# Softmax sums of an attention kernel on column quarters of the array: one reciprocal of 256 columns and eight products of 32 rows

## The chip, the cores and the metric

The kernel runs on one core of a Trainium2 chip. The metric is device time in microseconds (us) for one execution; the median of 3 runs of the kernel before is 2319.12 us (2315.53 to 2322.49).

## The reference

One transformer layer on x of 16 sequences x 512 tokens x 256 features, all in float32. First causal attention with 16 heads of 64 features, with the scores clamped by a tanh, and then a mixture of 8 experts (the best 2 of each token) beside one shared expert. Cut to what matters here:

```python
x = x + attn(layernorm(x));  x = x + ffn(layernorm(x))

def attn(x):                                  # per sequence: 512 tokens, 16 heads of 64
    q, k, v = (heads(x @ W.T) for W in (Wq, Wk, Wv))
    sim = 50 * tanh(q @ k.T / 8 / 50)
    attn = softmax(where(causal, sim, min))   # exp, divided by its sum over the keys
    return (attn @ v) @ Wo.T

def ffn(t):
    shared = gelu(t @ sw1 + sb1) @ sw2 + sb2
    p, i = top_k(softmax(t @ gate_w + gate_b), 2)
    routed = sum over the two of p * (gelu(t @ w1[i] + b1[i]) @ w2[i] + b2[i])
    return routed + shared
```

## The kernel before

**Attention.** Sequences (b, 0 to 15) and within each the eight pairs of heads (p, 0 to 7) are one stream of 128 steps. A pair's two heads (i = 0, 1) occupy partitions 0 to 63 and 64 to 127 wherever features lie on partitions. Scores are kept transposed: keys on partitions, queries along the free dimension, so the softmax sum over keys is a sum over partitions, which a product with a matrix of ones gives.

For each pair there are these parts. `project_qk` (L244) makes q and k with eight full-array matmul instructions of 512 columns (`pq`, L249; each float32 product is two instructions in the trace), copied to SBUF by ScalarE (L256). `score_matmuls` (L264) makes the scores in three units of key blocks, `s` at L272, with 64 rows of the array for either head. `exponentials` (L283) runs tanh and exp on ScalarE (L287, L288), masks the diagonal blocks on GpSimd (L291) and adds the key blocks of a pair on GpSimd (`added`, L303 to L310) for queries 128 to 511; for queries 0 to 127 only key block 0 counts. `attend` (L314) multiplies by the values into the PSUM tile `av` (L323; 64 columns of the array for either head), and then makes the sums, repeated over a head's 64 partitions, in the PSUM tile `sums` of 128 x 512 (L332). VectorE takes two reciprocals of 256 columns from `sums` into `oT` (L342) and multiplies `oT` by `av` over 512 columns (L343). `av` and `sums` have one buffer each, so the next pair's `av` matmuls can't begin before L343 has read this pair's.

**Order.** TensorE's order is written out by hand (L826 to L839): at step s come the score units 0 and 1 of the pair s + 1, then `attend` of the pair s, score unit 2 of s + 1, `early`, `project_qk` of s + 2, and `around`. The other engines' orders are made by a scheduler when the program is built; each engine works its own queue in order.

What stands between the attention steps depends on p. At p = 0 and 1 comes the output projection of the sequence before (`po`, L353), then at p = 1 its second layernorm. At p = 2 come the first layernorm of the next sequence (L186: statistics on VectorE, the power on GpSimd at L196, four normalising instructions on VectorE at L199) and values (`pv`, L232, copied out by VectorE at L239). At p = 3 and p = 5 `early` transposes a normalised sequence on TensorE (L214); VectorE copies one half to SBUF (L217) and ScalarE the other (L218). At p = 3 the shared expert's first product (`ph`, L695) and the gate (`pg`, L367) follow and read that copy, at p = 5 the values of the next sequence (`pv`, L232) do. At p = 4 comes `place` (L403): a running count of the chosen experts on VectorE, four dependent additions (`ahead`, L411), two small matmuls (`pos`, L414 and L415), `slot` on VectorE (L417), then the transpose of the gate's table (`pc`, L685), `pv`, and the shared expert's second product (`py`, L714, L722).

**Routed experts.** Sequences form two groups, of 9 and 6. When a group is complete, its routed tiles (`rT`, `rh`, `ry`, L577 to L612) are "fillers" between the steps, and after them the gather (`gather_steps`, L643): for each of 128 tokens, `acc` is loaded by SP's queue, two `part` tiles are fetched by indirect DMA that GpSimd issues (L653), and VectorE adds them weighted to `acc` (L668), which SP's queue then stores. Step i asks for its own two parts and then finishes step i - 1. `part` rotates through 4 buffers: a fetch waits until the addition of the part four before it is done. The 36 gather steps of the first group lie between attention steps, the 24 of the second at the end, beside the routed experts that the last sequence computes densely (L847 to L855).

## Time and profile before

| | |
|---|---|
| median of 3 runs | 2319.12 us |
| the profiled execution: its time | 2317.56 us |
| the profiled execution: its span | 2315.8 us |
| busy TensorE (matmul) | 2209.4 us, 95% |
| busy TensorE weight load | 1405.6 us, 61% |
| busy VectorE | 1102.8 us, 48% |
| busy ScalarE | 1037.9 us, 45% |
| busy GpSimd | 952.3 us, 41% |
| mean granted TensorE clock | 0.993 |

PE is TensorE's matmul, PEld its weight load, DVE is VectorE, ACT ScalarE, POOL GpSimd, and SP the engine whose queue issues most DMAs. A group's row gives line, engine, operation, output<-inputs, shapes and count, then busy time and mean duration of one in ns. In a row of the timeline the first number is the start in us from the span's start, the second the length of the stretch, and a bracket tells how long the engine idled before it and what ended that. The chain of waits is the work that ended last, followed back from the last instruction to whatever released it. Starts are recorded; the ends of matmuls are modelled, so a stage's length is read from its start to the next stage's start.

### The profile page before, as it was taken

The numbers are of one execution on the slowest core, as the hardware profiler recorded it, in microseconds if no ns is written. First come the engines' busy times: TensorE is split into PE (matmuls) and PEld (weight loads), VectorE is DVE, ScalarE is ACT, GpSimd is POOL, SyncE is SP. The second block draws the span as 40 slices with busy tenths as digits, with TensorE's granted clock in tenths as the row PEclk, the third lists the DMA queues.
The fourth block names the chain that finished last, engine by engine and source line by source line (L and its number), as shares of the span: only waits on it lengthen the run. The fifth ranks groups of instructions, "written<-read, shape, count | busy, mean of one in ns | idle before, by whom it ended". The sixth has DMA issues, their size and how long they took to land.

```text
span 2315.8 us, 29554 instructions
## 1 busy us (share of the span) xinstructions
PE 2209.4 (95%) x10968; PEld 1405.6 (61%) x10968; DVE 1102.8 (48%) x1858; ACT 1037.9 (45%) x1352; POOL 952.3 (41%) x1091
## 2 busy tenths in 40 slices
PE   7999999999999999999999999999999799899996
PEld 3555555556565555555667677667655465558874
DVE  3445454545363636363644434444446555453334
ACT  3544444444444545444444554554554444351211
POOL 3444443435353535344423412422455847450025
PEclk9999999999999999999999999999999999999999
DMA  5001010101010101010142342342230503035776
GB/s 191 1 1 37 1 37 1 37 1 37 1 37 1 37 1 37 1 37 1 37 147 59 118 128 64 101 128 82 84 97 20 153 7 119 21 100 168 224 228 208
DMA packets 119855, 161.34 MB, mean 70 GB/s; under 512 B 12320, under 2 KB 90144, under 8 KB 119200
## 3 DMA queue, kind: packets, MB, share of 16 engines
q1 hardware_dynamic: 107760, 125.62, 17.5%
q0 software_dynamic: 11520, 31.47, 4.4%
q10 hardware_dynamic: 432, 2.36, 0.3%
q8 instruction: 87, 1.43, 0.3%
q14 instruction: 56, 0.46, 0.1%
HBM read 99.64 MB, written 59.77 MB: 69 GB/s over the span
## 4 chain that ended last, share of the span: by engine, by line
PE 76%; DVE 11%; DMA 5%; issue 3%; ACT 3%; POOL 2%; SPq 0%; POOLq 0%; DVEq 0%; ACTq 0%
PE pq L249 15%; PE s L272 10%; PE av L323 10%; PE po L353 9%; PE pv L232 8%; PE ry L604 5%; PE rh L586 5%; DVE oT L342 4%; PE sums L332 4%; DMA part<-ys,packed 3%; PE ph L695 2%; PE py L714 2%; DVE xn_a L199 2%; PE pr L573 1%; PE py L722 1%
## 5 line engine op out<-in xcount | busy, mean ns | idle before, releaser
L287 ACT ACTIVATE pe<-s 128x768 f32<-128x768 f32 (+1 forms) x384 | 334.5, 874 | 704.8 <-PE s L272 679.1
L342 DVE RECIPROCAL oT<-sums 128x256 f32<-128x256 f32 x256 | 430.9, 1724 | 355.3 <-PE sums L332 355.2
L291 POOL TENSOR_SCALAR_AFFINE_SELECT pe<-pe 128x256 f32<-128x256 f32 (+1 forms) x384 | 192.0, 501 | 902.0 <-ACT pe L288 847.4
L272 PE MATMUL s<-qk 64*128 64x512 f32 (+3 forms) x2048 | 345.4, 456 | 11.9 <-ACT qk L256 11.5
L288 ACT ACTIVATE pe<-pe 128x768 f32<-128x768 f32 (+1 forms) x384 | 349.5, 914 | 10.9
L323 PE MATMUL av<-pe,v 128*64 128x512 f32 (+3 forms) x2048 | 307.8, 443 | 34.5 <-DVE oT L343 34.4
L272 PEld LDWEIGHTS s<-qk 64*128 64x128 f32 x2048 | 176.6, 186 | 200.7 <-issue 144.9
L323 PEld LDWEIGHTS av<-pe,v 128*64 128x64 f32 x2048 | 140.3, 138 | 241.7 <-issue 208.7
L249 PE MATMUL pq<-xT_a,wq_sb 128*128 128x512 f32 x512 | 252.8, 617 | 0.8 <-DVE xT_a L217 0.8
L249 PE MATMUL pq<-xT_a,wk_sb 128*128 128x512 f32 x512 | 241.6, 595 | 5.0 <-DVE x L360 3.5
L232 PE MATMUL pv<-wv_sb,xT_a 128*128 128x256 f32 x1024 | 233.6, 382 | 4.4 <-DVE xT_a L217 4.4
L303 POOL TENSOR_TENSOR added<-pe,pe 128x768 f32<-128x768 f32 x128 | 232.3, 1814 | 10.5
L256 ACT COPY qk<-pq 128x512 f32<-128x512 f32 x256 | 149.8, 585 | 178.0 <-PE pq L249 178.0
L232 PEld LDWEIGHTS pv<-wv_sb,xT_a 128*128 128x128 f32 x1024 | 195.1, 192 | 52.0 <-issue 24.4
L353 PE MATMUL po<-wo_sb,oT 128*128 128x256 f32 x1024 | 226.3, 380 | 0.0
L353 PEld LDWEIGHTS po<-wo_sb,oT 128*128 128x128 f32 x1024 | 195.2, 191 | 38.7 <-issue 14.3
L653 POOL DMA_INDIRECT part<-ys,packed x120 | 117.2, 977 | 154.4 <-DMA dw<-in_w 99.6
L249 PEld LDWEIGHTS pq<-xT_a,wk_sb 128*128 128x128 f32 x512 | 97.7, 191 | 129.1 <-issue 120.4
L595 ACT ACTIVATE rhT<-rh,biases 128x256 f32<-128x256 f32 x148 | 62.0, 470 | 253.5 <-PE rh L586 253.4
L307 POOL TENSOR_TENSOR added<-added,pe 128x512 f32<-128x512 f32 x128 | 163.5, 1277 | 10.7
L239 DVE COPY v<-pv 128x512 f32<-128x512 f32 x128 | 87.3, 689 | 144.9 <-PE pv L232 144.9
L586 PE MATMUL rh<-rT,ew 128*128 128x256 f32 x592 | 142.6, 385 | 6.3 <-DVE rT L577 5.5
(134 smaller groups left out, 2302.4 us busy)
## 6 DMA issues: line engine op xcount, KB each, us to landing
ew<-in_w SPq DMA_DIRECT2D x148, 256.0 KB, 3.1
rows<-xs SPq DMA_DIRECT2D x74, 256.0 KB, 3.1
ys<-y SPq DMA_DIRECT2D x74, 256.0 KB, 3.3
x<-in_x SPq DMA_DIRECT2D x16, 512.0 KB, 4.0
xs<-zeros SPq DMA_DIRECT2D x32, 256.0 KB, 4.3
kept<-x SPq DMA_DIRECT2D x15, 512.0 KB, 3.0
acc<-kept SPq DMA_DIRECT2D x60, 128.0 KB, 2.9
out<-acc SPq DMA_DIRECT2D x60, 128.0 KB, 2.4
```

What stands on the lines that cost most here:

```text
L232: nc.tensor.matmul(pv[:, u], xT[:, k, t * P : (t + 1) * P], wv_pairs[:, k, :, 2 * g : 2 * g + 2, :], start=(k == 0), stop=(k == KD - 1),)
L249: nc.tensor.matmul(pq, w[:, k, p * P : (p + 1) * P], xT[:, k, :], start=(k == 0), stop=(k == KD - 1),)
L272: nc.tensor.matmul(ps[:, i, at : at + w], qk[rows, 1, j * P : (j + 1) * P], qk[rows, 0, j * P :], start=True, stop=True,)
L287: nc.scalar.activation(pe[:, :, :w], ps[:, :, :w], AF.Tanh, scale=CLAMP_IN)
L288: nc.scalar.activation(pe[:, :, :w], pe[:, :, :w], AF.Exp, scale=SOFTCLAMP)
L291: nc.gpsimd.affine_select(out=diagonal, in_=diagonal, compare_op=ALU.is_ge, fill=0.0, base=0, pattern=[[0, 2], [0, n], [1, P]], channel_mu ...
L303: nc.gpsimd.tensor_tensor(added, pair_pe[b, p, 0][:, :, P:], pe[:, :, : N - P], ALU.add)
L307: nc.gpsimd.tensor_tensor(added[:, :, P:], added[:, :, P:], pe[:, :, : 2 * P], ALU.add)
L323: nc.tensor.matmul(po[i * DH : (i + 1) * DH, j * P :], v[:, j, i, p % 2, :], pair_pe[b, p, u][:, i, at : at + w], start=(j == 0), stop=(j ...
L342: nc.vector.reciprocal(oT[:, half], sums[:, half])
L353: nc.tensor.matmul(po[:, u, :], oTs[b, c][:, t * P : (t + 1) * P], wo_sb[:, c, :], start=(c == 0), stop=(c == NP - 1),)
L586: nc.tensor.matmul(ph[:, f, :], tile["w1"][:, d, f * P : (f + 1) * P], tile["T"][:, d, :], start=(d == 0), stop=(d == KD - 1),)
```

## The change

`sums` becomes 128 x 256. Its matrix of ones has 32 columns in place of 64, and every head has two quarters of 32 partitions: the first holds the sums of queries 0 to 255, the second those of queries 256 to 511. Eight products of 128 columns (two per quarter) take the place of four products (two of 128 and two of 384 columns); each is two instructions in the trace, as before. One reciprocal covers all of `sums` and is written to a new tile `rec` (one buffer). Since a quarter's 32 partitions serve 64 partitions of `av` and one half of the queries, the multiplication is cut into eight of 32 partitions x 256 columns; half of them read `rec` at another partition than they write. `part` has 3 buffers in place of 4.

```diff
+    Q = DH // 2
...
-        sums = ps_av.tile([P, N], F32, tag="sums", name=f"sums_{b}_{p}", bufs=1)
+        sums = ps_av.tile([P, N // 2], F32, tag="sums", name=f"sums_{b}_{p}", bufs=1)
...
-        for of, at, w in ((pair_pe[b, p, 0], 0, P), (pair_added[b, p], P, N - P)):
+        added = pair_added[b, p]
+        for c in range(2):
             for i in range(2):
-                nc.tensor.matmul(
-                    sums[i * DH : (i + 1) * DH, at : at + w],
-                    ones[:, :DH],
-                    of[:, i, :w],
-                    start=True,
-                    stop=True,
-                )
+                for h in range(2):
+                    at = (2 * h + c) * P
+                    nc.tensor.matmul(
+                        sums[i * DH + h * Q : i * DH + (h + 1) * Q, c * P : (c + 1) * P],
+                        ones[:, :Q],
+                        added[:, i, at - P : at] if at else pair_pe[b, p, 0][:, i, :P],
+                        start=True,
+                        stop=True,
+                    )
         oT = work.tile([P, N], F32, tag="oT", name=f"oT_{b}_{p}", bufs=NP + 2)
-        for h in range(2):
-            half = slice(h * (N // 2), (h + 1) * (N // 2))
-            nc.vector.reciprocal(oT[:, half], sums[:, half])
-        nc.vector.tensor_mul(oT, oT, po)
+        rec = work.tile([P, N // 2], F32, tag="rec", name=f"rec_{b}_{p}", bufs=1)
+        nc.vector.reciprocal(rec, sums)
+        for i in range(2):
+            for h in range(2):
+                for r in range(2):
+                    own = slice(i * DH + r * Q, i * DH + (r + 1) * Q)
+                    half = slice(h * (N // 2), (h + 1) * (N // 2))
+                    nc.vector.tensor_mul(
+                        oT[own, half], po[own, half], rec[i * DH + h * Q : i * DH + (h + 1) * Q]
+                    )
...
-                part = work.tile([P, D], F32, tag="part", name=f"part_{b}_{t}_{i}", bufs=4)
+                part = work.tile([P, D], F32, tag="part", name=f"part_{b}_{t}_{i}", bufs=3)
```

In the order that the scheduler makes of the changed kernel, three things move on VectorE. At p = 3 and p = 5 the copy L217, which stood between the reciprocals and the multiplication, stands behind the eight multiplications. At p = 4 two of the four `ahead` additions stood before the reciprocals, one between them and the multiplication, and one after; now none stands before the reciprocal, one between, and three after. On GpSimd some issues of `part` move by one to three places among the masks and additions.

## The prediction

> **What bounds the kernel now.** I read the busy shares first (TensorE 95%), then the chain of waits, then its stretch over one sequence, then the timeline around the sums, and last the groups of VectorE and of the gather.

> ```profile
> PE 76%; DVE 11%; DMA 5%; issue 3%; ACT 3%; POOL 2%; SPq 0%; POOLq 0%; DVEq 0%; ACTq 0%
> PE pq L249 15%; PE s L272 10%; PE av L323 10%; PE po L353 9%; PE pv L232 8%; PE ry L604 5%; PE rh L586 5%; DVE oT L342 4%; PE sums L332 4%; DMA part<-ys,packed 3%; PE ph L695 2%; PE py L714 2%; DVE xn_a L199 2%; PE pr L573 1%; PE py L722 1%
> ```

> TensorE carries the end, but not alone: the reciprocals hold as large a share (4%) as the sums that the change shortens. So VectorE, 48% busy, ends the path in places. The chain over one sequence shows two of them:

> ```profile
> 409.77 3.29 DVE oT L342 x2
> 413.05 0.02 issue
> 413.08 0.70 DVE oT L343
> 413.77 0.14 issue
> 413.91 2.38 PE av L323 x16
> ...
> 432.50 3.37 DVE oT L342 x2
> 435.87 0.04 DVE ahead L411
> 435.90 0.69 DVE oT L343
> 436.59 0.60 DVE ahead L411
> 437.19 0.02 issue
> 437.21 0.17 DVE ahead L409
> 437.38 0.15 DVE slot L417
> 437.54 0.04 issue
> 437.58 0.33 PE pc L685
> ```

> At p = 2 the next `av` waits for the multiplication that empties the one `av` buffer; at p = 4 `pc` waits for `slot`, which stands behind that multiplication. In all other pairs the work between two `av` stages covers VectorE: at p = 7, the shortest, 477.00 + 0.86 to 484.80 is 6.9 us.

> **The sums on TensorE.** Timeline at p = 5:

> ```profile
> 215.30 0.39 PE L332 MATMUL sums<-pe,ones 128*64 128x128 f32 x4
> 215.51 0.81 PE L332 MATMUL sums<-added,ones 128*64 128x384 f32 x4
> 216.26 0.92 PE L272 MATMUL s<-qk 64*128 64x256 f32 x8
> 217.11 1.09 PE L214 MATMUL pt_a<-ident,xn_a 128*128 128x128 f32 x8
> ```

> Full-array products set the rate: eight `pq` instructions of 512 columns take 3.44 us, so 0.43 us each and 0.107 for 128 columns. The four of 128 in `sums` take 0.21 us (215.30 to 215.51): the two halves run together. The stage is 0.213 + 0.640 = 0.853 us of stream; the chain has 0.86. After: eight products, sixteen instructions, of 128 columns. If four quarters run together that is 4 x 0.107 = 0.427 us; if still two, 0.853.

> The array's division now changes between `av` (64 columns) and `sums` (32), where both had the same. What a change of division costs: `s` of 256 and 128 columns streams 0.64 us and takes 0.85 (216.26 to 217.11), `sums` into `s` takes 0.96 in place of 0.85 (215.30 to 216.26), so 0.1 us of emptying and up to 0.1 us to load the first 128-column weights. With weights of 32 columns, a quarter of that: 0.1 + 0.025 = 0.125. Sums after: 0.55 us, a gain of 0.30 per pair; with two at a time a loss of 0.125. I take four: the halves show no cost for running side by side (0.853 of stream against 0.86 in the chain), and the program hands over quarters in the same alternation as halves. [...]

> Gain: 128 x 0.30 = 38.4 us, less 14 x 0.30 = 4.2 for the sums just ahead of the VectorE chain at p = 2, which doesn't start from them: **-34 us**.

> **VectorE.** One reciprocal is 1.69 us; two, 3.37. The product of 128 x 512 is 0.69. Eight products of 256 columns come in its place, and no row has 32 partitions. The nearest rows:

> ```profile
> 194.34 0.42 DVE L389 TENSOR_TENSOR eq<-pr 128x256 f32<-128x256 f32 x1
> 194.68 0.42 DVE L390 TENSOR_TENSOR gt<-pr 128x256 f32<-128x256 f32 x1
> 195.02 0.42 DVE L391 TENSOR_TENSOR eq<-eq,before 128x256 f32<-128x256 f32 x1
> 195.47 0.42 DVE L392 TENSOR_TENSOR gt<-gt,eq 128x256 f32<-128x256 f32 x1
> ```

> 256 columns last 0.42 us. Independent neighbours start 0.34 apart (194.34, 194.68); one that needs its predecessor starts 0.45 after it (195.02, 195.47). So eight cost 2.8 to 3.6 us. The 128 x 32 `slot` (0.19) would give 1.5, but it has fewer columns; I see no reason for fewer partitions to be faster. I take 0.43 each, 3.44: the overlap of neighbours is shown only between instructions on the same 128 partitions. [...]

> VectorE per pair: 3.35 + 0.04 + 0.69 = 4.08 before, 1.69 + 0.05 + 3.44 = 5.18 after, 1.10 longer. The halved reciprocal is more than given back. Where the 6.9 us cover it, that costs nothing. Where not, per sequence:

> - p = 2: `av` waits for this chain: 14 x 1.10 = 15.4 us. Queued behind it are only the `pv` copies, needed later.
> - p = 5: TensorE waits for the transposed half L217, which now stands behind the eight products. Before: sums end 216.26, and `pv` starts at 221.48, 5.22 us on, with no time lost. After: 0.12 to start + 5.18 + 0.63 for the copy, so 5.93, and `pv` at about 6.0: 0.8 late. 15 x 0.8 = 12.
> - p = 3: `ph` reads the same copy of the other normalisation: 15 x 0.8 = 12.
> - p = 4: before, `pc` starts 5.1 us after the sums end (432.45 to 437.58). After: products end at 5.3, two more `ahead` at 0.21 (the step of small dependent instructions, as from 192.53 to 192.75 in the timeline), `pos` 0.4, `slot` 0.2: 6.3. 15 x 1.2 = 18.

> Together **+57 us**. If the products overlap (2.8), these are 0.46, 0.15, 0.15 and 0.56: 6.4 + 2.25 + 2.25 + 8.4 = 19 us.

> **Three `part` buffers.** A fetch now waits for the addition three before it, and GpSimd is held meanwhile, with masks and `added` queued behind. In the tail the tile's rows show 48 fetches from 2237.1 to 2307.3 us, 1.5 us each, almost to the end of the program, so every delay counts. Issuing takes 0.96 + 0.30 = 1.26; landing is 3.6 us at the median and the addition 0.48, so one turn is 3.6 + 0.5 + 0.3 = 4.4 us: over four buffers 1.1, hidden by issuing, over three 1.47, not hidden. 48 x 0.2 = +10 us (nothing if the waits on `acc`, 15.4 us here, cover it; 24 if all additions come late). Between attention steps 72 fetches land after 3.1 us: 3.9 / 3 = 1.3 against 1.26, nearly nothing, except that an addition can stand behind the 5.2 us of a pair on VectorE. I take +8 (0 to 25). Sum **+18**. `rec` with one buffer costs nothing: reader and writer stand in one queue. SP's queue keeps its order.

> **Sum.** -34 + 57 + 18 = +41 on the profiled execution's 2317.56 (span 2315.8): **2359 us**, 1.8% slower. The median of before, 2319.12, is 0.07% off that.

> **Rivals.**
> - *Two quarters at a time.* Against it: halves side by side cost nothing. For it: no row has more than two. Sums lose 0.125 x 114 = 14: 14 + 57 + 18 = +89, 2407 us.
> - *Products overlap, all else as I say.* -34 + 19 + 18 = +3: 2321 us, no change.
> - *Faster.* One mechanism: products start 0.34 us apart, so that the transposed half is there when `pq` ends (4.66 + 0.63 = 5.3 against 5.22 us), and TensorE keeps its 34. -34 + 19 = -15, 2303 us, if three buffers cost nothing. For it: the overlap at L389 and L390. It decides below 0.36 us per product: four places then lose less than the sums gain.

> **How the numbers follow.** My forecast 0.50, two at a time 0.20, no change 0.15, faster 0.15. The range reaches from the faster case to two at a time, 2303 to 2408; about half of either's own spread lies beyond, under 0.2. This kernel's measurement tells 0.3% (7 us) from no change: faster 0.17, same 0.13, slower 0.70, for the middle cases spill over to both sides.

> **What would show it.** Sums: the stage at 0.55 us in the chain, starts of four at once; 0.85 to 1.0 tells of two. Products: the eight from start to start, 3.4 or 2.8. At p = 3 and 5, `ph` and `pv` waiting for L217; at p = 4, `pc` for `slot`; at p = 2, `av` for the products 1.1 us longer than 1.3. In the tail, the first to the last `part` 80 us in place of 70. The prediction fails most simply if products start well below 0.36 us apart, or if VectorE takes less time for 32 partitions.

## The result and the profile after

The changed kernel takes 2387.44 us (median of 4 runs, 2384.2 to 2395.51) against 2319.94 for the kernel before (4 runs): a ratio of 1.0302, 95% interval 1.0276 to 1.0329, so 3.0% slower. The profiled execution took 2389.79 us, its span 2388.1, against 2317.56 and 2315.8: 72 us more where +41 was forecast. The time lies inside the range, the sign is right, the size is not.

From the page of the kernel after, the busy shares, the chain that ended last, and the new group on VectorE:

```profile
PE 2214.9 (93%) x11992; PEld 1408.2 (59%) x11992; DVE 1239.3 (52%) x2626; ACT 1035.3 (43%) x1352; POOL 949.5 (40%) x1091
PE 76%; DVE 12%; issue 4%; DMA 3%; ACT 2%; POOL 2%; another core or an unknown queue 1%; SPq 0%; POOLq 0%; ACTq 0%; DVEq 0%
L351 DVE TENSOR_TENSOR oT<-av,rec 32x256 f32<-32x256 f32 x1024 | 430.3, 420 | 15.8
```

TensorE is busy 5.5 us longer than before, although the sums became shorter. That is the first sign of something beside waiting, since a wait adds no busy time. VectorE is busy 136 us longer: 128 pairs of 1.07 us. A product of 256 columns on 32 partitions takes 420 ns, like the rows of 128 partitions in the forecast (0.42 us).

The chain of waits over one sequence (start, duration, what) shows the places named in the forecast: p = 2, then p = 3, then p = 4:

```profile
424.54 3.75 PE av L324 x16
428.29 0.57 PE sums L336 x16
428.86 0.85 PE s L273 x8
...
430.74 3.45 PE pq L250 x8
434.19 0.02 issue
434.21 0.70 DVE x2T_f L218
434.91 0.14 issue
435.05 3.67 PE ph L705 x8
...
446.81 0.84 DVE ahead L421
447.65 0.33 DVE oT L351
...
451.06 0.18 DVE ahead L421
...
452.17 3.72 PE pv L233 x16
```

Four things are to be seen. The sums take 0.57 us. `ph` waits for the copy x2T_f, which stands behind the eight products. At p = 4 a dependent `ahead` of 0.84 us stands between the reciprocal and the products. And `av`, once it may start, takes 3.75 us where the chain of before had 2.38 for the same 16 instructions.

The last point is told by the clock. Two neighbouring stretches of the kernel after (the columns: from and to, the length, the busy time and instructions of TensorE, its weight load, VectorE, ScalarE and GpSimd, then the granted clock, the DMA share and GB/s):

```profile
420.99:424.40 3.41, 0.78 (x6) 0.16 (x2) 3.31 (x8) 3.11 (x4) 0.42 (x1) 0.93 0.00 0
424.40:427.81 3.41, 3.27 (x12) 1.41 (x14) 1.29 (x2) 0.51 (x1) 2.22 (x2) 0.57 0.00 0
```

While TensorE waits 2.77 us for the products (0.78 us busy of 3.41), the clock is still nearly full; in the stretch after it, in which `av` runs, the mean is 0.57. The trace's records of the granted clock hold only full rate and half rate (0.50); the half rate here goes from 423.93 to 427.35, so it begins 0.6 us before `av` does. Over the whole execution the mean granted clock is 0.978 against 0.993. Read as time at half rate this is 2 x 0.022 x 2388 = 105 us, against 2 x 0.007 x 2316 = 32 before.

**One sequence added up.** From one output projection to the next, a sequence without fillers between its steps took 117.5 us before (eight of them, called plain below); after, 122.4 in five of the eight and about 124 in three, 123.0 in the mean. For one of 122.4:

| | forecast | measured |
|---|---|---|
| p = 2, longer wait of `av` | +1.10 | +1.18 |
| p = 2, `av` at half clock (3.75 - 2.38) | nothing | +1.37 |
| p = 3, wait, and a slower `ph` (3.67 for 3.43) | +0.80 | +0.88 + 0.24 |
| p = 4, wait, and a slower `pv` (3.72 for 3.46) | +1.20 | +1.70 + 0.26 |
| p = 5, wait, and a slower `pv` (3.81 for 3.46) | +0.80 | +0.88 + 0.35 |
| seven `sums`, 0.29 shorter each | -2.1 | -2.0 |
| together | +1.8 | +4.9 |

In the row of p = 2, TensorE's own wait (the bracket in these rows of its timeline, before and after) grew by more, from 1.31 to 2.77 us, as the sums ahead of it end 0.29 us earlier; that part is not lost.

```profile
413.91 2.38 PE L323 MATMUL av<-pe,v 128*64 128x512 f32 x16 [1.31 <-DVE oT L343]
424.54 3.75 PE L324 MATMUL av<-pe,v 128*64 128x512 f32 x16 [2.77 <-DVE oT L351]
```

At p = 4 this sequence has an `ahead` of 0.93 us in its own row, of which the chain counts 0.84. In the other seven it lasts 0.65 us and the wait is about 0.3 us shorter. The runs don't show what stretches this addition of 128 x 8, which took 0.10 us between the reciprocals and the product in the kernel before.

The half rate hits more often in some sequences than in others. In the eight plain ones of the kernel after, TensorE waits 2.77 us at p = 2 every time and the clock halves after seven of these waits; the waits at p = 4, 1.6 us in seven sequences, are followed by it four times. The five sequences with one such stretch take 122.2 to 122.4 us, the three with two 124.1. One stretch more in the same program costs 1.7 us.

**The whole kernel added up.** Eight such sequences: 8 x 5.5 = +44. A ninth, 142.3 us before: +4. Three whose steps hold routed fillers (170, 170, 159.5 before): +3.5 together, as no wait of `av` shows in TensorE's rows there (1180 to 1690 us in the kernel after). Two with gather steps (135.7, 133.1 before): +14. The first and the last: -2 and +2. The tail from the first to the last `part`, 70.2 to 78.1: +8. Together +73, for 72 measured.

### The profile page after: what moved, and what is told of

Read it like the earlier page. It is cut to its first block, busy times and chain, and to the rows that moved or that the text cites. A ratio compares the mean times of both kernels' runs of the same rounds, so it can differ in the third digit from the quotient of the medians.

```text
span 2388.1 us, 32411 instructions
## 1 busy us (share of the span) xinstructions
PE 2214.9 (93%) x11992; PEld 1408.2 (59%) x11992; DVE 1239.3 (52%) x2626; ACT 1035.3 (43%) x1352; POOL 949.5 (40%) x1091
## 3 DMA queue, kind: packets, MB, share of 16 engines
q10 hardware_dynamic: 432, 2.36, 0.3%
## 4 chain that ended last, share of the span: by engine, by line
PE 76%; DVE 12%; issue 4%; DMA 3%; ACT 2%; POOL 2%; another core or an unknown queue 1%; SPq 0%; POOLq 0%; ACTq 0%; DVEq 0%
PE pq L250 14%; PE av L324 11%; PE s L273 11%; PE po L363 9%; PE pv L233 9%; PE ry L614 5%; PE rh L596 5%; DVE oT L351 4%; PE ph L705 3%; PE sums L336 3%; DVE rec L345 2%; DVE xn_a L200 2%; PE py L724 2%; PE pr L583 1%; PE pg L377 1%
## 5 line engine op out<-in xcount | busy, mean ns | idle before, releaser
L351 DVE TENSOR_TENSOR oT<-av,rec 32x256 f32<-32x256 f32 x1024 | 430.3, 420 | 15.8
L345 DVE RECIPROCAL rec<-sums 128x256 f32<-128x256 f32 x128 | 224.7, 1756 | 329.7 <-PE sums L336 323.6
L324 PE MATMUL av<-pe,v 128*64 128x512 f32 (+3 forms) x2048 | 318.7, 455 | 33.5 <-DVE oT L351 33.5
L233 PE MATMUL pv<-wv_sb,xT_a 128*128 128x256 f32 x1024 | 254.9, 405 | 29.2 <-DVE xT_a L218 20.0
L233 PEld LDWEIGHTS pv<-wv_sb,xT_a 128*128 128x128 f32 x1024 | 204.4, 203 | 91.9 <-issue 44.9
L250 PEld LDWEIGHTS pq<-xT_a,wk_sb 128*128 128x128 f32 x512 | 97.8, 191 | 127.2 <-issue 122.9
```

The costliest lines, as they stand in the source:

```text
L233: nc.tensor.matmul(pv[:, u], xT[:, k, t * P : (t + 1) * P], wv_pairs[:, k, :, 2 * g : 2 * g + 2, :], start=(k == 0), stop=(k == KD - 1),)
L250: nc.tensor.matmul(pq, w[:, k, p * P : (p + 1) * P], xT[:, k, :], start=(k == 0), stop=(k == KD - 1),)
L324: nc.tensor.matmul(po[i * DH : (i + 1) * DH, j * P :], v[:, j, i, p % 2, :], pair_pe[b, p, u][:, i, at : at + w], start=(j == 0), stop=(j ...
L345: nc.vector.reciprocal(rec, sums)
L351: nc.vector.tensor_mul(oT[own, half], po[own, half], rec[i * DH + h * Q : i * DH + (h + 1) * Q])
```

## The experiments

**Three buffers alone.** The kernel before, with one number changed.

```diff
-                part = work.tile([P, D], F32, tag="part", name=f"part_{b}_{t}_{i}", bufs=4)
+                part = work.tile([P, D], F32, tag="part", name=f"part_{b}_{t}_{i}", bufs=3)
```

> The kernel before with three part buffers in place of four and nothing else changed: the third part of the change alone. My theory prices it at +18 us (10 in the tail, 8 between attention steps): 2337 to 2338. Rival: the gather waits on its acc loads anyway, and three buffers cost nothing: 2317 to 2322. If it is 30 us or more, the change's loss lies here and not on VectorE.

Measured: 2331.55 us, ratio 1.0046 (1.0029 to 1.0062), so +11 us. From the row of `part` in the tail:

```profile
L653 POOL DMA_INDIRECT part<-ys,packed x48: 954/960/1207, 2244.7 to 2321.6; - x48
```

2244.7 to 2321.6 is 76.9 us, against 70.2 before: 7 us in the tail and some 4 between the steps, where the two gather sequences grew by 6.8 and 3.5 us and others shrank. The step of the forecast holds at two thirds of its size.

**One product in place of eight.** The kernel after with one multiplication over 512 columns; the right mapping of quarters to queries is left out.

```diff
-        for i in range(2):
-            for h in range(2):
-                for r in range(2):
...
+        nc.vector.tensor_mul(
+            oT.rearrange("p (h c) -> p h c", h=2),
+            po.rearrange("p (h c) -> p h c", h=2),
+            rec.unsqueeze(1).to_broadcast([P, 2, N // 2]),
+        )
```

> The changed kernel with the eight products replaced by one of 128 x 512 that reads rec twice (it leaves out that a quarter of rec serves the other 32 partitions of its head, so half of the products take another sum). Sums on quarters, the one reciprocal and three part buffers stay. If the loss comes from the eight products (VectorE late for av, the transposed copies and slot, and what TensorE's clock does after such waits), VectorE per pair falls from 5.2 to 2.5 us, all of these waits go, the half-clock stretches fall from 109 us to about the 33 of before, and it is faster than before: 2319 - 38 (128 x 0.30) - 15 to 25 (what VectorE is ahead of before at p = 2 and p = 4) + up to 18 for part = 2262 to 2300. If the loss came from the sums or from part, it stays above 2340.

Measured: 2277.01 us, ratio 0.9811 (0.9795 to 0.9828): 110 us less than the kernel after. At p = 2, in its chain, `av` follows the scores at once:

```profile
402.40 2.38 PE av L324 x16
```

A sequence takes 113.9 us. The quarters, the single reciprocal and the three buffers together are a gain of 44 us; the eight products are the whole loss, and more.

**The wait of p = 2 filled with idle matmuls.** The kernel after, with six matmuls that nobody reads (they write `sums`, which the real sums overwrite) in front of `av` of p = 3. The wait stays; TensorE doesn't idle in it.

```diff
+        if p == 3 and 1 <= b < B - 1:
+            for _ in range(6):
+                nc.tensor.matmul(sums, ident, wo_sb[:, 0, :], start=True, stop=True)
```

> The changed kernel, with six idle matmuls of 128 x 256 (2.6 us, into the sums tile, which the true sums overwrite) added for 14 sequences at the place where TensorE waits 2.8 us for the products before av of p = 3. It adds work and removes no wait. Theory: the wait lets the granted clock fall to half for one stretch of 3.41 us, in which av takes 3.75 in place of 2.38 us; kept busy, the clock stays, and 14 x 1.4 = 19 us go: 2368 to 2375. Rival: the long av is the late buffer or a slow restart, not the clock: 2387 to 2395, no gain, or slightly slower for the added work.

Measured: 2392.47 us, ratio 1.0311 (1.0294 to 1.0328), no gain. In its chain:

```profile
418.52 2.79 PE sums L322 x12
421.31 2.36 PE av L327 x16
...
447.56 5.41 PE pv L233 x16
```

`av` is back at 2.36 us, so its 3.75 did come from TensorE's idling, and not from anything in `av`. But in the same sequence `pv` after the wait of p = 4 now takes 5.41 us in place of 3.72. In five of the eight plain sequences a half-rate stretch follows the wait of p = 4; these take 122.4 to 122.7 us, the three without one 120.7. So eleven stretches became five, all behind the next wait, and the plain sequences took 1.2 us less each. The ninth and those with fillers, where the idle matmuls fill no wait, took 13 us more and used that up. The part of my expectation that concerned `av` held; the one that concerned the total fell.

**All four waits filled.** The same with 6, 2, 4 and 2 idle matmuls at p = 2, 3, 4 and 5:

```diff
+        if 3 <= p <= 5 and done >= 0 and b < B - 1:
+            busy(b, p + 1, (2, 4, 2)[p - 3])
```

> The changed kernel with idle matmuls of 128 x 256 into the next sums tile in all four waits: six ahead of av of p = 3, two ahead of ph at p = 3, four ahead of pos at p = 4, two ahead of pv at p = 5. With the first place alone av got quick (2.36 us) but the half-clock stretch moved to pv after the wait of p = 4. Theory (the clock falls after a stretch of 3.41 us in which TensorE idled about half or more, wherever it lies): with no long wait left in sequences 1 to 14, their half-clock stretches go, the half clock falls from 109 us to 50 to 65, and (109 - 57) / 2 = 26 us are won though work was added and no wait taken away: 2355 to 2370. Rival: the clock isn't what costs, and it stays at 2385 to 2400.

Measured: 2380.15 us, ratio 1.0271 (1.0253 to 1.0288), 7 us less than the kernel after. The mean granted clock:

```profile
core 0: 2376.8 us, clock 0.990
```

Time at half rate falls from 105 to 2 x 0.010 x 2377 = 48 us. The eight plain sequences take 120.8 us instead of 123.0: 8 x 2.2 = 17 us back, and none of them has a half-rate stretch. That agrees with the eleven stretches of the kernel after at 1.7 us each. The ninth sequence and those with fillers, where the idle matmuls lie in nobody's wait, take 0.9 to 4.0 us more, and that eats 9 of the 17. So the clock is a cause, of some 17 us in the plain sequences; as a cure, idle work is poor.

The slower products behind a wait are another matter. In the same chain the idle matmuls (`sums`, L326) run right up to `ph` at p = 3 and to `pv` at p = 5:

```profile
428.54 0.86 PE sums L326 x4
429.41 3.67 PE ph L720 x8
...
465.33 0.86 PE sums L326 x4
466.21 3.81 PE pv L233 x16
```

3.67 and 3.81 us are what the kernel after has. So it isn't idling that makes these stages long, but the data that come late. In the trace of the kernel before, the instructions of one stage overlap those of the next: one of 512 columns lasts 0.59 us and the next starts 0.43 us after it, with its weights loaded in between (from 221.05 for the `pv` that starts at 221.48). Behind a wait for the copy, the first weights are loaded only when the copy is there (at 435.01 in the kernel after, the copy ending at 434.91 and `ph` starting at 435.05), and that overlap is lost once.

**Both copies on ScalarE.** The kernel after, with the half of the transposed sequence that VectorE copied given to ScalarE, so that `ph` and `pv` need nothing from behind the products.

```diff
-        nc.vector.tensor_copy(xT[:, 0, :], pt[:, 0])
+        nc.scalar.copy(xT[:, 0, :], pt[:, 0])
```

> The changed kernel with the first half of the transposed copy also on ScalarE, so that it stands no longer behind the eight products on VectorE at p = 3 and p = 5. Theory: the waits of ph and pv (0.9 us each, and 0.24 to 0.35 to start again) go, and with them some half-clock stretches: 15 x 2.3 = 35 us, 2345 to 2360. Rival: ScalarE's own queue (tanh and exp of the next pair) makes both halves late instead, and it is 2385 or more.

Measured: 2352.32 us, ratio 1.0134 (1.0117 to 1.0151), 35 us less than the kernel after. In its chain `ph` of p = 3 and `pv` of p = 5 follow `pq` at once and run at their old lengths:

```profile
427.88 3.43 PE ph L705 x8
...
463.29 3.45 PE pv L233 x16
```

The table above has 1.12 + 1.23 = 2.35 us for these two places. The eight plain sequences took 120.5 us, 2.5 less each: the two waits are confirmed in place and nearly in price, with the longer stage behind each of them. That 15 x 2.35 = 35 us gives the whole difference as well is partly chance: the other sequences changed by -6.6 to +2.3 us.

**The products ordered by quarter.** The kernel after with the two products of one quarter next to each other, and `rec` read at the quarter that is written; the sums used are the wrong ones for half of the queries.

```diff
-            for h in range(2):
-                for r in range(2):
+            for r in range(2):
+                for h in range(2):
...
-                    nc.vector.tensor_mul(
-                        oT[own, half], po[own, half], rec[i * DH + h * Q : i * DH + (h + 1) * Q]
-                    )
+                    nc.vector.tensor_mul(oT[own, half], po[own, half], rec[own])
```

> The changed kernel with the eight products in the order head, quarter, half, each reading rec on the same 32 partitions as it writes (it leaves out that rec of the other quarter is wanted, so half of the sums are wrong). Theory: an instruction whose operands start on other partitions than its predecessor's waits for that one's end; now the second of each two starts on the same: four of the eight start 0.34 us after their predecessor, four 0.43, 3.1 us in place of 3.44, and at some 50 uncovered places 0.35 us are won: about 2370. Rival: 32-partition instructions never overlap: 3.44 us and 2388. Second rival: reading rec at another partition was what cost: all at 0.34, 2.8 us.

Measured: 2352.25 us, ratio 1.0147 (1.0129 to 1.0166), 35 us less. In its timeline of VectorE at p = 2:

```profile
413.62 3.07 DVE L351 TENSOR_TENSOR oT<-av,rec 32x256 f32<-32x256 f32 x8
```

Eight take 3.07 us; the same row of the kernel after has 3.46. One lasts 0.42 us, and the starts are alternately 0.345 and 0.42 us apart: two of one quarter overlap here, two of different quarters do not. The time at half rate fell as well, to 2 x 0.014 x 2348 = 66 us: the wait of `av` at p = 2 is now 2.38 us, and only one of the eight plain sequences still has a half-rate stretch, where the kernel after has eleven in them. They take 119.4 us, 3.6 less each. Four places of 0.39 us and ten stretches of 1.7 us in eight sequences make 3.7.

**Sums on halves again.** The kernel after with the sums on 64 columns of the array per head; those of queries 0 to 255 are overwritten and so left out.

```diff
-                for h in range(2):
-                    at = (2 * h + c) * P
...
+                nc.tensor.matmul(
+                    sums[i * DH : (i + 1) * DH, to : to + w],
+                    ones[:, :DH],
```

> The changed kernel with the sums made by halves of 64 columns again, 0.853 us of stream, written over one another into the same 128 x 256 tile (it leaves out the sums of queries 0 to 255, which are overwritten); reciprocal, products and part as in the changed kernel. Theory: the quarters win 0.29 us per pair, of which 7 of 8 pairs count: 113 x 0.29 = 33 us, so 2415 to 2425. Rival: the quarters win nothing on the path, and it stays at 2388.

Measured: 2409.93 us, ratio 1.0389 (1.037 to 1.0408): 22 us more than the kernel after. In its chain the stage is as long as it was before the change:

```profile
430.23 0.87 PE sums L336 x12
```

So the quarters do shorten the stage by 0.30 us. What that is worth on the path this run doesn't show: the eight plain sequences took 122.9 us, no more than the 123.0 of the kernel after, although seven stages of 0.30 us were added. They have five half-rate stretches in place of eleven (the wait at p = 2 is 2.48 us here), and the wait at p = 4 is shorter, 1.1 for 1.6 us, with `ahead` in another place of VectorE's order. Of the 22 us, 11 lie in one sequence with gather steps.

**The waits moved out of the way.** The kernel after with `rec` in the right half of `oT`, which makes room for the fourth `part` buffer, both copies on ScalarE, the values of p = 4 ahead of `place`, and the next sequence's first layernorm at p = 0 in place of p = 2, so that its 4.4 us of normalising no longer stand ahead of the products.

```diff
-        rec = work.tile([P, N // 2], F32, tag="rec", name=f"rec_{b}_{p}", bufs=1)
+        rec = oT[:, N // 2 :]
...
+        if p == 0 and more:
+            xns[b + 1, 0] = layernorm(x_tiles[b + 1], f"a{b + 1}")
...
-            if more:
-                xns[b + 1, 0] = layernorm(x_tiles[b + 1], f"a{b + 1}")
...
+            if b < B:
+                project_v(b, 3, xTs[b])
             if done >= 0:
```

> Correct, with quarters, one reciprocal and eight products as in the changed kernel, but with the waits that they made taken away: rec lies in the second half of oT, so part keeps four buffers; both halves of the transposed copy go to ScalarE; at p = 4 the values are projected ahead of place; the first layernorm of the next sequence moves from p = 2 to p = 0, where 6.9 us of po cover it. Theory: TensorE waits at none of the four places, its clock stays up, and what is left is the gain of the sums: 2319 - 37 (128 x 0.29) - 18 (14 waits of 1.3 us that the kernel before had at p = 2) - 5 (0.3 us at p = 4) = 2259, 2250 to 2285. Rival: VectorE (5.2 us per pair) is late at yet other places, and it is above 2319.

Measured: 2292.76 us, ratio 0.9887 (0.9871 to 0.9904): faster than both kernels, 95 us below the kernel after, but 8 us above the range I expected and 34 above its middle. At p = 4 `pos` now follows the values' copy, which stands behind the products, so moving `pv` ahead filled the wait only in part. But little is lost there; from the list of what TensorE waited for (us in total, times, longest):

```profile
PE av L324 <- POOL added L309: 20.5, 3, 9.4
PE pos L424 <- DVE v L240: 2.0, 10, 0.2
```

The plain sequences take 114.6 us, 3.0 less than in the kernel before, where the expectation has 3.9. Most of what is missing lies elsewhere: three waits of `av` for GpSimd's `added`, 20.5 us, and the three sequences with fillers, which gained nothing.

**The same without the layernorm's move.**

```diff
-        if p == 0 and more:
-            xns[b + 1, 0] = layernorm(x_tiles[b + 1], f"a{b + 1}")
...
+            if more:
+                xns[b + 1, 0] = layernorm(x_tiles[b + 1], f"a{b + 1}")
```

> The version with the waits moved (2293 us) with the layernorm put back to p = 2: the one wait of p = 2 alone, on quarters with eight products. Theory: 2.8 us of TensorE idle in one piece per sequence without fillers, of which 2.4 are lost, and after it a half-clock stretch that costs 1.4 in most of them: (2.4 + 1.4) x 9 = 34, 2318 to 2330. Rival without the clock: 2.4 x 9 = 22 us or less, 2305 to 2315.

Measured: 2320.68 us, ratio 1.0 (0.9992 to 1.0009), as expected. The one wait at p = 2, with the half rate behind it, is worth 28 us, or 26 by the ratios. In its chain:

```profile
414.17 3.47 PE av L324 x16
417.64 1.01 PE sums L336 x16
```

In each of the eight plain sequences `av` waits 2.85 to 2.87 us; six of them have a half-rate stretch and take 119.1 us, two have none and take 117.5. The same wait with and without the half rate: 1.6 us are the clock's.

**What the moves are worth without the change.** Two kernels made from the one before: the first with the layernorm's move alone,

```diff
+        if p == 0 and more:
+            xns[b + 1, 0] = layernorm(x_tiles[b + 1], f"a{b + 1}")
...
-            if more:
-                xns[b + 1, 0] = layernorm(x_tiles[b + 1], f"a{b + 1}")
```

the second with it, the values of p = 4 ahead of `place`, and the copies on ScalarE:

```diff
-        nc.vector.tensor_copy(xT[:, 0, :], pt[:, 0])
+        nc.scalar.copy(xT[:, 0, :], pt[:, 0])
...
+            if b < B:
+                project_v(b, 3, xTs[b])
             if done >= 0:
```

> The kernel before, with only the first layernorm of the next sequence moved from p = 2 to p = 0. Theory: the 1.3 us that av waits at p = 2 go: 14 x 1.3 = 18 us, 2298 to 2306. Rival: the normalisation delays something else at p = 0, and it stays within 2312 to 2322.

> The control for the version in which the waits were moved (2293 us): the same moves (layernorm to p = 0, both copies on ScalarE, values ahead of place) on the kernel before, with sums on halves, two reciprocals and one product. Theory: the moves give 18 to 25 us here too, 2294 to 2302, so that the quarters with their eight products are worth less than 10 us even where their waits are moved. Rival: the quarters are worth their full 0.29 us per pair there, 37 us, and this one is near 2320.

Measured: 2302.45 us, ratio 0.9926 (0.9913 to 0.9939), and 2308.41, ratio 0.995 (0.9937 to 0.9963); the first within its expectation, the second above. With the old sums, the other two moves lose 6 us. So of the 26 us that the moved kernel with quarters gains on the one before, 17 can be had without the change. Quarters with halved reciprocal add (0.9926 - 0.9887) x 2320 = 9 us to the best kernel on halves, and 15 us where all the moves are the same.

## Why the prediction was right or wrong

- **Sums, right.** "Sums after: 0.55 us" was 0.57, and 0.85 on halves. Four instructions of a stage start within 0.02 us in the timeline; two of the rows:

```profile
428.22 0.30 PE L336 MATMUL sums<-pe,ones 128*32 128x128 f32 x1
428.24 0.30 PE L336 MATMUL sums<-added,ones 128*32 128x128 f32 x1
```

  The rival "two quarters at a time" is out. The 0.125 us for the change of division came out within 0.02, but its parts were not measured apart, and "a quarter of that" for weights of 32 columns isn't borne out: in the traces such a load lasts 0.11 us, one of 64 columns 0.14 and one of 128 columns 0.19. So this match is partly luck.
- **Products, right.** 0.43 us from start to start, 3.46 for eight, VectorE 5.17 us a pair at p = 2 (419.23 to 424.40) for 5.18. The rivals "products overlap" and "faster" are out: overlap was seen only within a quarter (starts 0.345 us apart in the products ordered by quarter).
- **The four places, right in place.** All four waits came. At p = 4 "two more `ahead`" after the products was right, but the one ahead of them was counted at nothing: 1.7 us in the sequence shown and 1.4 in the others, not 1.2. And in that sequence it is `pos` that waits for `ahead`, and `pv` for `slot`; `pc`, which was to wait for `slot`, starts before `slot` does.
- **The price of a wait, wrong.** This is the step that failed. "14 x 1.10" and the three terms beside it count the length of the wait alone. A wait cost TensorE more here, in two ways. After many of the longer waits the granted clock halved for 3.41 us: +1.37 us on `av` at p = 2 in the sequence shown, 1.6 to 1.7 for a stretch where sequences of one program with and without it can be compared. The idle matmuls show that idling causes it, and the 17 us of the filled waits are its size in the plain sequences. And a stage that waited for its data took 0.24 to 0.35 us longer at full clock, whether TensorE idled or not; without the wait this goes (both copies on ScalarE). The clock could have been looked for before: the mean clock of 0.993 stood in the table of before, and the wait of 1.31 us that `av` already had left it at 2.38 us. That nothing of this showed at 1.31 us was no reason to carry the price on to 2.77.
- **"15 x" and "14 x", wrong in the other direction.** Sequences with routed fillers lose 0.5 to 1.7 us, not the same as the others.
- **Three buffers, right in kind.** +11 for +18: 7 in the tail for 10, about 4 between the steps for 8.

By kind: 9 sequences without fillers cost 48 us where the forecast had 9 x 1.8 = 16. For eight of them the difference, 3.65 us each, can be divided: eleven half-rate stretches of 1.7 us are 2.3, the longer stages behind three waits 0.85, and the `ahead` with 0.08 at each of the other three waits makes up the rest. The three with fillers cost 3.5 for 5.4, and the gather sequences with the tail 22 for 22. That these agree so well is partly chance, as single sequences among them moved by several us from kernel to kernel. What stays open is how the clock's part divides over the sequences with fillers, gather steps and the tail, and why `ahead` grew.

## What to carry to other kernels

Price a wait of the busiest engine as its length plus what the engine loses when it starts again, and look at the granted clock of the stretch behind the longest wait of the trace before scaling it up. Splitting one instruction into pieces of fewer partitions saved VectorE nothing here: eight pieces of 32 partitions took 3.46 us (kernel after) where one of 128 took 0.69 (kernel before), so a shorter sum on one engine must first be paid for on the other. When an off-path engine gets longer, count which instructions in its queue the bounding engine needs; moving those (a copy, a layernorm) was worth more here than the sums.
